# An output projection begun one block earlier beside a state-space scan, and GpSimd's pair addition kept to two blocks

## The chip, the core and the metric

The kernel runs on one core of a Trainium2 chip. The engines named here are TensorE (PE, matrix products; PEld are its weight loads), VectorE (DVE), ScalarE (ACT), GpSimd (POOL) and SyncE (SP), which issues most DMAs. Each works through its own instructions in the order in which the program gives them. The metric is device time of one execution in microseconds; lower is better.

## The reference

Four blocks follow each other on `x` of 2 x 512 rows of 512 numbers, each with a layer norm ahead and another behind, and a residual sum. Cut to the parts that matter here:

```python
x = x + ln(scan_block(ln(x)))      # the change is here
x = x + ln(gptq_ffn(ln(x)))        # ... and at the beginning of this
x = x + ln(attention(ln(x)))
x = x + ln(latent_ffn(ln(x)))

def scan_block(h):
    x, gate = split(h @ W_in.T)                    # 1024 channels each
    x = silu(causal_conv(x))
    ts, B, C = split(x @ W_x.T)                    # ranks: 32, 16, 16 wide, RMS-normed
    dt = softplus(ts @ W_dt.T + b_dt)
    state_t = state_{t-1} * exp(dt_t * A) + (dt_t * x_t) * B_t     # 16 states a channel
    y_t = sum_n(state_t * C_t)
    return ((y + x * D) * silu(gate)) @ W_out.T    # the output projection

def gptq_ffn(h):                                    # weights in 4 bits, 512 -> 1376 -> 512
    g, u = h @ Wg, h @ Wu
    return (silu(g) * u) @ Wd
```

## The kernel before

**Tiling.** A batch's 512 rows are four tiles of 128 rows (`TB` = 4) for norms and residual sums; for the scan, channels are on the partitions and time runs along the free axis. 2 batches of 8 channel blocks (`NCH` = 8, 128 channels each) make 16 blocks k; each has 8 steps gi (`NGI` = 8) of two states (`NG` = 2), so 128 steps s.

**Stages.** The first stage (to about 68 us) makes norms, projections and the convolution of batch 0. The second is the loop over s that is described next. The third (from L1180) projects batch 1's output, finishes the FFN of batch 0 and goes on to the rest of the model.

**A step of the scan.** VectorE multiplies (dt u) by B for two states (`times_B`, L1073) and runs the recurrence over 1024 elements (`scan`, L1077); ScalarE makes the decay factors two steps ahead (`exps`, L1057) in PSUM; GpSimd multiplies the states by C (`times_C`, L1083), and in the steps that `paired` names it adds the two states to each other (L1085). Two steps later TensorE sums the states into `y` in PSUM by products with the identity (`sums`, L1105): two products of 512 columns, or one where GpSimd has added already. Two steps into the next block VectorE multiplies `g` by `y` (`fin`, L1111). A product of 512 columns is two records of 0.43 us in the profile.

B and C of batch 1 are loaded step by step over block 7 (`states`, L560): each C tile is issued when GpSimd has read the buffer's last use by batch 0.

**The stream beside it.** Everything else that TensorE does in the second stage comes from one generator, `stream`: gates of batch 0, projections and ranks of batch 1, gates of batch 1, the product of two weight matrices of the last FFN (`fc1_expert`, stored to `wfe_d`), the output projection of batch 0 (`out_tiles`), the transposes of its norm (`turned`) and the FFN's first half (`ffn0`, 11 chunks of gate and up, 8 products each). Each step gives it a budget (`STEP` = 3.5 us, a product counts `MM` = 0.86) and takes products from it until that is used. `yield MM` ends a product; `until(key, lag)` holds the stream until an event lies `lag` half steps back. The clock `now` counts half steps (`tick`, two a step).

**Jobs.** What follows a product on the other engines is a job, given with `spawn(job, lag)` and advanced by `tick`; its `yield n` puts n half steps between its instructions. `bank` hands out the two PSUM buffers of the stream in turn, and `release` marks their last use. `pin` then fixes the order of TensorE, ScalarE, VectorE and GpSimd as it was written; SP's is the order of its DMAs in the program.

**The output projection.** For each tile i, 8 products over the blocks c go into one bank, with weights from four loads of 512 KB (`wo_pair`, L917; three buffers, shared with other weights). `out_job` evicts the bank, takes the moments (`add_normed`), normalizes, adds to `x` on GpSimd (L910), and `norm_one` starts the FFN's norm, whose result `turned` transposes for `ffn0`. `ffn_up_job` (L990) multiplies silu(gate) by up on VectorE.

In the third stage batch 1's projection (L1194) runs beside the dequantization of the down weights (`once`, L328 and L329, stored to `wd_d`), and the down projection (L1216) loads them from there.

Of the kernel before, what the change touches and what calls it, by code (L numbers as in the profile page):

```python
# [18 lines left out]
P = 128  # L19
# [4 lines left out]
TB = S // P  # L24
# [32 lines left out]
def tile_sandwich(  # L57
# [58 lines left out]
    def moments(srcs, name):  # L116

        mv = stat.tile([P, TB, 2], F32, tag="mv", name=f"mv_{name}")
        for i, s in enumerate(srcs):
            st = stat.tile([P, 6], F32, tag="st", name=f"st_{name}_{i}")  # L120
            nc.vector.bn_stats(st, s)
            nc.vector.bn_aggr(mv[:, i, :], st)
        return mv
# [304 lines left out]
    with ExitStack() as mamba:  # L428
# [254 lines left out]
        with ExitStack() as p2:  # L683
# [24 lines left out]
            def spawn(gen, lag=0):  # L708
                jobs.append([now[0] + lag, gen])
# [87 lines left out]
            def until(key, lag):  # L797
                while st.get(key, 1 << 30) + lag > now[0]:
                    yield None
# [32 lines left out]
            def turned(name, dst):  # L832

                for i in range(TB):
                    yield from until((name, i), 2)
                    tp = yield from bank(f"tp_{name}_{i}")
                    tp = tp.rearrange("p (k t) -> p k t", k=KH)
                    for kc in range(KH):
                        nc.tensor.transpose(tp[:, kc, :], st[name, i, "xn"][:, ts(kc, P)], ident)

                    def out(i=i, tp=tp):
                        nc.scalar.copy(dst[:, :, ts(i, P)], tp)
                        release(f"tp_{name}_{i}")
                        st[name, i, "free"] = st[name, "out"] = now[0]
                        yield 1

                    spawn(out(), 2)
                    yield MM / 2
                for i in range(TB):
                    while (name, i, "free") not in st:  # L850
                        yield None
# [31 lines left out]
                spawn(out(), 2)  # L883
                yield MM / 2

            def norm_one(b, i, name):

                mv = moments([xs(b)[i]], f"{name}_{i}")
                rs = rstd(mv, f"{name}_{i}", 1)
                nm = minus_mean(mv, rs, f"{name}_{i}", 1, True)  # L890
                yield 4
                xn = jrow(f"xn_{name}_{i}")
                apply(
                    xn.rearrange("p (k a r) -> p r k a", k=KH, a=2),
                    xs(b)[i].rearrange("p (r k a) -> p r k a", k=KH, a=2), rs, nm, 0,
                )
                st[name, i] = now[0]
                st[name, i, "xn"] = xn

            def add_normed(b, i, src, o):  # L900

# [13 lines left out]
            def wo_pair(b, i, j):  # L915
                w = wst.tile([P, 2, H], F32, tag="w4", name=f"wo{b}_{i}_{j}")
                nc.sync.dma_start(out=w, in_=w_out[j])  # L917
                return w

            def out_job(i, ps):  # L920
                o = jrow(f"o0_{i}")
                if i < TB - 1:
                    nc.scalar.copy(o, ps)
                    release(f"po0_{i}")
                    yield 3
                    yield from add_normed(0, i, o, o)
                else:
                    yield from add_normed(0, i, ps, o)
                    release(f"po0_{i}")
                yield 1  # L930
                yield from norm_one(0, i, "f0")

            def fc1_expert():

                fT = w4(fc1_wT.rearrange("p k (a n) -> p (k a) n", n=PW), "wf1T")
                fT = fT.rearrange("p (k a) n -> p k (a n)", k=LAT // P)
                ex = w4(expert_w, "wex", LAT // P, LAT)
                for a in range(KH // 2):
                    ps = yield from bank(f"pfe{a}")
                    for e in range(2):  # L940
                        for k in range(LAT // P):
                            nc.tensor.matmul(
                                ps[:, ts(e, LAT)], fT[:, k, ts(2 * a + e, P)], ex[:, k, :],
                                start=(k == 0), stop=(k == LAT // P - 1),
                            )
                        yield MM

                    def out(a=a, ps=ps):
                        t_ = trow(f"fe{a}")
                        nc.scalar.copy(t_, ps)  # L950
                        release(f"pfe{a}")
                        nc.sync.dma_start(
                            out=wfe_d[:, 2 * a : 2 * a + 2, :].rearrange("p k n -> p (k n)"), in_=t_
                        )
                        yield 1

                    spawn(out(), 2)

            def out_tiles():
                yield from until("fin7", 0)  # L960
                todo = [(i, j) for i in range(TB) for j in range(NCH // 2)]
                ws = {}
                for n, (i, j) in enumerate(todo):
                    for m in range(n, min(n + 2, len(todo))):
                        if m not in ws:
                            ws[m] = wo_pair(0, *todo[m])
                    if j == 0:
                        ps = yield from bank(f"po0_{i}")
                    for e in range(2):
                        c = 2 * j + e  # L970
                        nc.tensor.matmul(  # L971
                            ps, g[0][c][:, ts(i, P)], ws[n][:, e, :],
                            start=(c == 0), stop=(c == NCH - 1),
                        )
                        yield MM
                    if j == NCH // 2 - 1:
                        spawn(out_job(i, ps), 2)

            its = {}

# [29 lines left out]

            def stream():
                for c in range(1, NCH):
                    yield from gate(0, c)
                xT.append(xT_tile("xT1"))
                w_in(0, 1, 0)
                yield from turned("n1", xT[1])
                for c in range(NCH):
                    yield from proj_x(c)
                yield from until("words", 2)
                yield from gate(1, 0)  # L1020
                yield from gate(1, 1)
                yield from ranks1()
                yield from gate(1, 2)
                yield from gate(1, 3)
                yield from rows1()
                for c in range(NCH - 4, NCH):
                    yield from gate(1, c)
                yield from fc1_expert()
                yield from out_tiles()
                hTs["f", 0] = xT_tile("hT_f0")  # L1030
                yield from turned("f0", hTs["f", 0])
                yield from ffn0()
# [54 lines left out]
            def paired(s):  # L1087

                k, gi = divmod(s, NGI)

                return order[k][0] == 1 and (k - NCH not in (2, 3) and gi in (1, 5) or k - NCH < 2 and gi % 2 == 1)

            def sums(s):
                k, gi = divmod(s, NGI)
# [403 lines left out]
```

## Time and profile before

| | us |
|---|---|
| three runs | 945.83, 949.47, 949.53 (median 949.47) |
| the profiled execution | 946.45 |
| its span | 944.5 |
| first scan to the last scan's end | 68.0 to 562.1 |
| busy TensorE | 859.0 (91% of the span) |
| busy VectorE | 666.7 (71%) |
| busy GpSimd | 487.0 (52%) |
| busy ScalarE | 429.2 (45%) |
| mean granted clock of TensorE | 0.968 |

The first scans of the blocks from 6 on begin at 261.9, 292.0, 320.0 (block 8, the first of batch 1), 350.4, 386.4, 418.4, 447.5, 477.9, 506.9 and 536.5 us. The profile lists one execution; a line of the groups gives source line, engine, operation, tiles, count, then busy time, mean nanoseconds of one, and the idle time just before with what ended it. A row of the timeline has the start, the length, the engine, the line and the tiles, and in brackets the idle time before it and what was waited for. The windows give busy time (and instructions) of each engine in a stretch, then the granted clock of TensorE, the DMA share and GB/s.

### The profile page before, as it was taken

The page shows a single profiled execution, that of the slowest core. Times are in us where ns is not written, and L with a number is a line of the kernel's source. Part 1 is how long each engine was busy: PE and PEld are TensorE (multiplying, and loading weights), DVE is VectorE, ACT ScalarE, POOL GpSimd, SP SyncE. Part 2 cuts the span into 40 slices and gives each one's busy share as a digit, 9 for nine tenths or more (in the row PEclk, how much of TensorE's full clock was granted, in tenths as well). Part 3 has the DMA queues.
Part 4 walks back from the last instruction along what each step waited for, and adds up shares of the span by engine and source line. Part 5 has one row for each costly group of instructions (what it writes and reads, how often), then busy time and mean ns, then how long its engine had stood idle before and what let it go on. Part 6 is the DMA issues. An engine that isn't in the chain of part 4 may idle for free.

```text
span 944.5 us, 7179 instructions
## 1 busy us (share of the span) xinstructions
PE 859.0 (91%) x2188; PEld 384.5 (41%) x2188; DVE 666.7 (71%) x768; ACT 429.2 (45%) x655; POOL 487.0 (52%) x358
## 2 busy tenths in 40 slices
PE   6989979879999899579999999898999998999994
PEld 3434433323544343234434434344544444445441
DVE  5778999999999998999999986425600034535235
ACT  3368875655667645575565530215220014422122
POOL 7758887767887777866788783520000000011012
PEclk9989999989999899799999999999999999999998
DMA  6649100110004855000011114345212221200101
GB/s 195 207 135 375 38 30 31 38 38 25 21 25 169 287 173 158 25 0 23 22 44 45 31 32 145 132 138 200 67 57 88 59 90 44 67 12 23 56 0 44
DMA packets 43816, 80.08 MB, mean 85 GB/s; under 512 B 7774, under 2 KB 20937, under 8 KB 43778
## 3 DMA queue, kind: packets, MB, share of 16 engines
q1 hardware_dynamic: 41506, 73.64, 23.8%
q0 software_dynamic: 1984, 5.47, 1.6%
q10 hardware_dynamic: 288, 0.52, 0.2%
q8 instruction: 17, 0.28, 0.1%
q14 instruction: 21, 0.17, 0.1%
HBM read 68.37 MB, written 11.24 MB: 84 GB/s over the span
## 4 chain that ended last, share of the span: by engine, by line
PE 52%; DVE 25%; issue 8%; POOL 5%; ACT 4%; DMA 1%; DVEq 0%; POOLq 0%; SPq 0%; ACTq 0%
DVE bx L1077 9%; PE py L1105 8%; DVE bx L1073 7%; PE pd L1426 6%; PE pup L1363 5%; PE fo L1216 4%; PE fu L373 3%; PE fo L1279 3%; PE fg L373 3%; PE fu L1002 3%; PE po L1194 3%; PE fg L1002 3%; POOL bx L1083 3%; PE po L971 2%; DVE u L485 2%
## 5 line engine op out<-in xcount | busy, mean ns | idle before, releaser
L1083 POOL TENSOR_TENSOR bx<-bx,C 128x1024 f32<-128x1024 f32 x128 | 301.7, 2358 | 105.5 <-DVE bx L1077 84.2
L1077 DVE TENSOR_TENSOR_SCAN bx<-da,bx 128x1024 f32<-128x1024 f32 x128 | 292.1, 2283 | 0.3 <-ACT da L1057 0.2
L1105 PE MATMUL py<-bx,ident 128*128 128x512 f32 x480 | 233.7, 617 | 31.3 <-POOL bx L1083 26.6
L1057 ACT ACTIVATE da<-dt,A 128x511 f32<-128x511 f32 x256 | 176.4, 690 | 146.2 <-DVE bx L1077 140.3
L1073 DVE TENSOR_TENSOR bx<-du,B 128x1024 f32<-128x1024 f32 x127 | 153.4, 1209 | 3.6 <-POOL bx L1085 1.5
L1105 PEld LDWEIGHTS py<-bx,ident 128*128 128x128 f32 x480 | 90.9, 196 | 157.3 <-issue 93.6
L387 POOL TENSOR_TENSOR sd<-ve,half 128x4 f16<-128x4 f16 x2 | 2.1, 1042 | 110.7 <-DVE ve L385 110.7
L1292 DVE TENSOR_TENSOR it<-it,fu 128x512 f32<-128x512 f32 (+1 forms) x11 | 7.6, 687 | 72.3 <-PE fu L373 72.3
L1363 PE MATMUL pup<-hT_l,wup 128*128 128x512 f32 x128 | 57.8, 607 | 0.0
L749 PE MATMUL pg<-xT,w_g 128*128 128x512 f32 x114 | 56.2, 624 | 0.7 <-ACT dt L573 0.7
L1426 PE MATMUL pd<-wdn,hid 128*128 128x512 f32 x128 | 55.3, 592 | 0.0
L129 POOL TENSOR_TENSOR rs_lo<-ve_lo,mhalf 128x1 f32<-128x1 f32 x8 | 5.4, 680 | 76.7 <-DVE ve_lo L127 76.7
L1216 PE MATMUL fo<-wd,it 128*128 128x512 f32 (+1 forms) x88 | 39.7, 615 | 2.6 <-DMA wd<-wd_d 2.6
L1002 PE MATMUL fg<-hT_f,wg 128*128 128x512 f32 (+1 forms) x88 | 42.1, 597 | 0.0
L485 DVE SCALAR_TENSOR_TENSOR u<-px,ch,u 128x511 f32<-128x511 f32 (+2 forms) x48 | 35.9, 747 | 7.6 <-ACT u L478 6.5
L373 PE MATMUL fg<-hT_f,wg 128*128 128x512 f32 (+1 forms) x88 | 40.2, 593 | 0.7 <-ACT hT_f L173 0.7
L1002 PE MATMUL fu<-hT_f,wu 128*128 128x512 f32 (+1 forms) x88 | 40.7, 592 | 0.0
L373 PE MATMUL fu<-hT_f,wu 128*128 128x512 f32 (+1 forms) x88 | 39.8, 593 | 0.0
L1279 PE MATMUL fo<-wd,it 128*128 128x512 f32 (+1 forms) x88 | 39.6, 592 | 0.0
L1426 PEld LDWEIGHTS pd<-wdn,hid 128*128 128x128 f32 x128 | 24.2, 190 | 30.7 <-issue 30.1
L1291 ACT ACTIVATE it<-fg 128x512 f32<-128x512 f32 (+1 forms) x11 | 6.6, 597 | 65.7 <-PE fg L373 65.7
L1363 PEld LDWEIGHTS pup<-hT_l,wup 128*128 128x128 f32 x128 | 24.3, 193 | 28.8 <-issue 28.8
(242 smaller groups left out, 1165.8 us busy)
## 6 DMA issues: line engine op xcount, KB each, us to landing
wo<-in_W_outT SPq DMA_DIRECT2D x20, 512.0 KB
B<-scr SPq DMA_DIRECT2D x16, 512.0 KB
C<-scr SPq DMA_DIRECT2D x16, 512.0 KB
wg<-wgu_d SPq DMA_DIRECT2D x10, 512.0 KB
wu<-wgu_d SPq DMA_DIRECT2D x10, 512.0 KB
w_x<-in_W_in SPq DMA_DIRECT2D x8, 512.0 KB
wgu_d<-w_gu POOLq DMA_DIRECT2D x16, 256.0 KB, 2.4
w_g<-in_W_in SPq DMA_DIRECT2D x8, 512.0 KB
```

The source lines that it names most:

```text
L373: nc.tensor.matmul(ps[:m], w[:, kc, e * P : e * P + m], hT[:, kc, :], start=(kc == 0), stop=(kc == KH - 1),)
L749: nc.tensor.matmul(ps, w[:, k, ts(e, P)], xT[b][:, k, :], start=(k == 0), stop=(k == KH - 1))
L1002: nc.tensor.matmul(ps[:m], wt[j][a][:, kc, e * P : e * P + m], hT[:, kc, :], start=(kc == 0), stop=(kc == KH - 1),)
L1057: nc.scalar.activation(das[s % 2][:, i, 1:], st["dt", b, c][:, 1:], AF.Exp, scale=A[:, c, n : n + 1])
L1073: nc.vector.tensor_mul(bx, st["du"].unsqueeze(1).to_broadcast([P, NG, S]), Bbs[b][gi])
L1077: nc.vector.tensor_tensor_scan(flat, das[s % 2].rearrange("p n t -> p (n t)"), flat, 0.0, ALU.mult, ALU.add)
L1083: nc.gpsimd.tensor_mul(bxs[s], bxs[s], Cbs[b][s % NGI])
L1105: nc.tensor.matmul(st["y"], ident, bx[:, i, :], start=False, stop=last)
L1216: nc.tensor.matmul(fo[t], its[i][:m, ts(t, P)], w[:m, e], start=(i == 0), stop=(i == len(IC) - 1),)
L1279: nc.tensor.matmul(fo[t], its[i][:m, ts(t, P)], w[:m], start=(i == 0), stop=(i == len(IC) - 1),)
L1363: nc.tensor.matmul(ps, w[:, kc, ts(e, P)], src[kc], start=(kc == 0), stop=(kc == KH - 1))
L1426: nc.tensor.matmul(pd, hid[kc][:, ts(i, P)], wdn[kc], start=(kc == 0), stop=(kc == INT // P - 1),)
```

## The change

It has four parts, all in the second stage:

1. `fc1_expert` and its stores move from behind the gates of batch 1 to behind those of batch 0; its weights are loaded by `fc1_weights` one gate earlier.
2. The output projection of batch 0 starts when block 6 is finished (`fin6`), not block 7. Tile 1 goes first, over blocks 0 to 6, in a bank `pp0_1` that ScalarE copies to `po0_part`; then tile 0, whose last product waits for `fin7`; then tile 1's part is brought back by a product with the identity and block 7 is added. Tiles 2 and 3 follow.
3. Tiles 2 and 3 go through `late_tile`: the moments are read from PSUM, the lags between the instructions are shorter, and the sum with `x` is on VectorE. In `turned`, the lag for these tiles is 1 half step rather than 2.
4. `paired` names the odd steps of blocks 8 and 9 alone. Before, it also named steps 1 and 5 of blocks 12 to 15.

```diff
             def turned(name, dst):
                 for i in range(TB):
-                    yield from until((name, i), 2)
+                    lag = 1 if name == "f0" and i >= TB - 2 else 2
+                    yield from until((name, i), lag)
                     tp = yield from bank(f"tp_{name}_{i}")
                     tp = tp.rearrange("p (k t) -> p k t", k=KH)
                     for kc in range(KH):
...
                         st[name, i, "free"] = st[name, "out"] = now[0]
                         yield 1
-                    spawn(out(), 2)
+                    spawn(out(), lag)
                     yield MM / 2
                 for i in range(TB):
                     while (name, i, "free") not in st:
...
                 spawn(out(), 2)
                 yield MM / 2
-            def norm_one(b, i, name):
-                mv = moments([xs(b)[i]], f"{name}_{i}")
-                rs = rstd(mv, f"{name}_{i}", 1)
-                nm = minus_mean(mv, rs, f"{name}_{i}", 1, True)
-                yield 4
+            def spread_out(b, i, name, rs, nm):
                 xn = jrow(f"xn_{name}_{i}")
                 apply(
                     xn.rearrange("p (k a r) -> p r k a", k=KH, a=2),
...
                 )
                 st[name, i] = now[0]
                 st[name, i, "xn"] = xn
+            def norm_one(b, i, name):
+                mv = moments([xs(b)[i]], f"{name}_{i}")
+                rs = rstd(mv, f"{name}_{i}", 1)
+                nm = minus_mean(mv, rs, f"{name}_{i}", 1, True)
+                yield 4
+                spread_out(b, i, name, rs, nm)
             def add_normed(b, i, src, o):
...
                 nc.sync.dma_start(out=w, in_=w_out[j])
                 return w
+            def late_tile(i, ps, o):
+                mv = moments([ps], f"mo0_{i}")
+                rs = rstd(mv, f"mo0_{i}", 1)
+                nm = minus_mean(mv, rs, f"mo0_{i}", 1, True)
+                yield 2
+                apply(o, ps, rs, nm, 0)
+                release(f"po0_{i}")
+                yield 1
+                nc.vector.tensor_add(xs(0)[i], xs(0)[i], o)
+                mv = moments([xs(0)[i]], f"f0_{i}")
+                rs = rstd(mv, f"f0_{i}", 1)
+                nm = minus_mean(mv, rs, f"f0_{i}", 1, True)
+                yield 2
+                spread_out(0, i, "f0", rs, nm)
             def out_job(i, ps):
                 o = jrow(f"o0_{i}")
-                if i < TB - 1:
-                    nc.scalar.copy(o, ps)
-                    release(f"po0_{i}")
-                    yield 3
-                    yield from add_normed(0, i, o, o)
-                else:
-                    yield from add_normed(0, i, ps, o)
-                    release(f"po0_{i}")
+                if i >= TB - 2:
+                    yield from late_tile(i, ps, o)
+                    return
+                nc.scalar.copy(o, ps)
+                release(f"po0_{i}")
+                yield 3
+                yield from add_normed(0, i, o, o)
                 yield 1
                 yield from norm_one(0, i, "f0")
-            def fc1_expert():
+            def fc1_weights():
                 fT = w4(fc1_wT.rearrange("p k (a n) -> p (k a) n", n=PW), "wf1T")
                 fT = fT.rearrange("p (k a) n -> p k (a n)", k=LAT // P)
-                ex = w4(expert_w, "wex", LAT // P, LAT)
+                return fT, w4(expert_w, "wex", LAT // P, LAT)
+            def fc1_expert(fT, ex):
                 for a in range(KH // 2):
                     ps = yield from bank(f"pfe{a}")
                     for e in range(2):
...
                     spawn(out(), 2)
             def out_tiles():
-                yield from until("fin7", 0)
-                todo = [(i, j) for i in range(TB) for j in range(NCH // 2)]
+                yield from until(f"fin{NCH - 2}", 0)
+                todo = [(i, j) for i in (1, 0, *range(2, TB)) for j in range(NCH // 2)]
                 ws = {}
+                def add(ps, i, c, w, start=False):
+                    nc.tensor.matmul(
+                        ps, g[0][c][:, ts(i, P)], w[:, c % 2, :],
+                        start=start, stop=(c == NCH - 1 - (i == 1 and "part" not in st)),
+                    )
+                def part_out(ps):
+                    part = st["part"] = new_u("po0_part")
+                    nc.scalar.copy(part, ps)
+                    release("pp0_1")
+                    st["parted"] = now[0]
+                    yield 1
                 for n, (i, j) in enumerate(todo):
                     for m in range(n, min(n + 2, len(todo))):
                         if m not in ws:
                             ws[m] = wo_pair(0, *todo[m])
                     if j == 0:
-                        ps = yield from bank(f"po0_{i}")
-                    for e in range(2):
-                        c = 2 * j + e
-                        nc.tensor.matmul(
-                            ps, g[0][c][:, ts(i, P)], ws[n][:, e, :],
-                            start=(c == 0), stop=(c == NCH - 1),
-                        )
+                        ps = yield from bank(f"pp0_{i}" if i == 1 else f"po0_{i}")
+                    for c in (2 * j, 2 * j + 1):
+                        if c < NCH - 1:
+                            add(ps, i, c, ws[n], start=(c == 0))
+                            yield MM
+                    if j < NCH // 2 - 1:
+                        continue
+                    if i == 1:
+                        spawn(part_out(ps), 2)
+                        continue
+                    yield from until(f"fin{NCH - 1}", 0)
+                    add(ps, i, NCH - 1, ws[n])
+                    yield MM
+                    spawn(out_job(i, ps), 2)
+                    if i == 0:
+                        yield from until("parted", 0)
+                        ps = yield from bank("po0_1")
+                        nc.tensor.matmul(ps, ident, st["part"], start=True, stop=False)
                         yield MM
-                    if j == NCH // 2 - 1:
-                        spawn(out_job(i, ps), 2)
+                        add(ps, 1, NCH - 1, ws[n])
+                        yield MM
+                        spawn(out_job(1, ps), 2)
             its = {}
...
             def stream():
                 for c in range(1, NCH):
+                    if c == NCH - 1:
+                        fw = fc1_weights()
                     yield from gate(0, c)
                 xT.append(xT_tile("xT1"))
                 w_in(0, 1, 0)
+                yield from fc1_expert(*fw)
                 yield from turned("n1", xT[1])
                 for c in range(NCH):
                     yield from proj_x(c)
...
                 yield from rows1()
                 for c in range(NCH - 4, NCH):
                     yield from gate(1, c)
-                yield from fc1_expert()
                 yield from out_tiles()
                 hTs["f", 0] = xT_tile("hT_f0")
                 yield from turned("f0", hTs["f", 0])
...
                 k, gi = divmod(s, NGI)
-                return order[k][0] == 1 and (k - NCH not in (2, 3) and gi in (1, 5) or k - NCH < 2 and gi % 2 == 1)
+                return NCH <= k < NCH + 2 and gi % 2 == 1
             def sums(s):
                 k, gi = divmod(s, NGI)
```

## Prediction, made before the changed kernel was run

> **What bounds the kernel now.** The busy table gives TensorE 91% of the span and VectorE 71%, but the 40 slices show VectorE at 9 tenths from about 140 to 540 us, where the scan runs. The groups say what a step of the scan holds:
>
> ```profile
> L1077 DVE TENSOR_TENSOR_SCAN bx<-da,bx 128x1024 f32<-128x1024 f32 x128 | 292.1, 2283 | 0.3 <-ACT da L1057 0.2
> ...
> L1073 DVE TENSOR_TENSOR bx<-du,B 128x1024 f32<-128x1024 f32 x127 | 153.4, 1209 | 3.6 <-POOL bx L1085 1.5
> ```
>
> Scan and times_B together are 3.49 us by the means; successive scans start 3.31 us apart (records overlap a little), so a block of 8 steps with its du (0.87) and fin (0.6) takes 27.95 us. Next, what VectorE itself waits for between 68 and 562 us (the view of waits: total, times, longest):
>
> ```profile
> DVE g L1111 <- PE py L1105: 4.5, 2, 3.4
> DVE du L1071 <- ACT du L1065: 2.7, 2, 1.9
> DVE st_f L121 <- POOL x L910: 1.9, 2, 1.5
> DVE it L990 <- PE fu L1002: 1.8, 2, 1.3
> DVE bx L1073 <- POOL bx L1085: 1.5, 1, 1.5
> ```
>
> Under 13 us of 494: **the scan is VectorE-bound**, and each microsecond put on VectorE, or each new wait of VectorE, moves the end of the scan. The change can win these waits, or lose by new ones. Last, the timeline where block 7 ends and the output projection begins (start, length, instruction; SPq is the load queue):
>
> ```profile
> 317.35 1.98 PE L1105 MATMUL py<-bx,ident 128*128 128x512 f32 x4 [0.79 <-POOL bx L1083]
> ...
> 321.53 0.32 SPq L560 DMA_DIRECT2D C<-scr  x1
> 321.55 3.66 PE L1105 MATMUL py<-bx,ident 128*128 128x512 f32 x4 [2.22 <-POOL bx L1083]
> ...
> 325.52 0.66 DVE L1111 TENSOR_TENSOR g<-g,py 128x512 f32<-128x512 f32 x1
> ...
> 327.86 4.51 PE L971 MATMUL po<-wo,g 128*128 128x512 f32 x6 [1.59 <-DMA wo<-in_W_outT]
> ```
>
> The last C tile of batch 1 goes out at 321.53, when GpSimd has read the buffer for the last time; the first `wo` is right behind it in SP's queue (321.94) and is used at 327.86. The fin of block 7, at 325.52, waits for nothing.
>
> **A. The early start: +6.3.** In the changed order, tile 1's projection over blocks 0 to 6 (7 products) fills TensorE in block 7, where it idles; then comes tile 0's first product, and only behind it the last two `sums` of block 7. SP takes its queue in order: B and C tiles of batch 1 now stand between the `wo` loads, and the load for tile 0 still stands behind the last C. It therefore issues at about 321.9 as before and lands at about 328.2 (327.7 before by its semaphore, and I add 0.5 because two 512 KB loads replace two 256 KB stores ahead of it). TensorE is in order, so the last `sums` of block 7 wait for a load that they do not need. Then 0.86 us for tile 0's product (two records of 0.43) and 1.72 for the sums, plus 0.2 to drain: fin of block 7 at 331.0. Behind fin on VectorE stand times_B and the scan of block 8, then ScalarE's exponentials and GpSimd's products. 331.0 is +5.5.
>
> Here the clock decides the rest. The row at 321.55 took 3.66 us for four records which took 1.98 at 317.35, after 2.22 us idle, and the windows give
>
> ```profile
> 320.00:325.00 5.00, 3.45 (x4) 1.18 (x4) 5.00 (x4) 3.05 (x4) 3.85 (x2) 0.66 0.93 290
> ```
>
> with a granted clock of 0.66 (third number from the end). The Trainium skill, "TensorE: Matmul & The Clock Gate", section "Part 1: The HAM clock gate", has half clock after an idle window of about 3.4 us; the new wait, from about 323 to 328.2, is longer than that, the old 2.22 is not and yet it was followed by half clock. So the row is the stricter. By full clock +5.5; with both products at half clock 328.2 + 1.7 + 3.66 = 333.6, +8.1. I take +6.3, fin at 331.8.
>
> **B. Waits that go: -4.5.** The 1.47 (times_B behind GpSimd's pair addition at 337.6) and the 3.42 (fin of block 8, at 360.27) exist because TensorE came late into block 8. From 328.2 it has 35 products to the last `sums` of block 8, before 36 from 327.86, so it gets there at about 360.1 again; fin of block 8 is due at 360.27 - 3.42 - 1.47 + 6.3 = 361.7. Both waits go, -4.9. The moments of tile 2, now read from PSUM with a shorter lag, wait some 0.4. Both ends: -4.9 and 0.
>
> **C. Residual additions of tiles 2 and 3 from GpSimd to VectorE: +0.6.** Two 128x512 additions at 0.65 (fin's row, 0.66) are +1.3. The trace has no such addition in the scan, with both inputs in SBUF: du, y and the exponentials are in PSUM. The nearest rows are from the dequantization:
>
> ```profile
> 582.55 0.68 DVE L328 TENSOR_TENSOR w_d<-q_d,z_d 128x512 f32<-128x512 int32 x1
> ...
> 583.31 1.39 POOL L329 TENSOR_TENSOR w_d<-w_d,s_d 128x512 f32<-128x512 f32 x1 [0.96 <-DVE w_d L328]
> ...
> 583.60 1.65 DVE L328 TENSOR_TENSOR w_d<-q_d,z_d 128x512 f32<-128x512 int32 x1
> ```
>
> Alone 0.68; begun inside a GpSimd operation of 1.39 it ends just after it (585.25 against 584.70). The rule that speaks against the change is in "SBUF — State Buffer", section "SBUF: two separate sides": VectorE with two SBUF inputs and GpSimd share a port pair as an exclusive lock, and the second blocks for all of the first's instruction. The row agrees in kind. By the row each addition loses 1.0; by the rule, against GpSimd's times_C of 2.36 us, up to 2.4 each; nothing if GpSimd is idle there, as it is some 20% of this stretch. I take 0.6 each, the low side since the step's order lets times_C finish first: +1.2. The waits of VectorE's norms on GpSimd's additions go, -1.9. Range -0.6 to +4.2.
>
> **D. One more FFN product inside the scan, and its waits: +5.4.** Everything comes 8 half steps earlier, so ten of eleven `it` products run on VectorE inside the scan, not nine: +0.6. What these wait for is the greater part. Before, one fu product finishes in the same step as the `it` that reads it, and it costs:
>
> ```profile
> 464.10 1.21 DVE L1073 TENSOR_TENSOR bx<-du,B 128x1024 f32<-128x1024 f32 x1
> ...
> 466.62 0.69 DVE L990 TENSOR_TENSOR it<-it,fu 128x512 f32<-128x512 f32 x1 [1.31 <-PE fu L1002]
> ```
>
> A second (436.18, one step of lag) costs 0.50. In the changed order five (numbers 0, 2, 7, 8, 9) stand in the step of their last product. Four at about 1.1 and the first at 2.2 (TensorE starts the FFN cold) are 6.6, less the 1.8 measured: +4.8. This holds while TensorE has no lead, and it has none: the first 10 FFN blocks, the sums and projections from block 10 on are 193 products, 193 x 0.859 = 165.8 us, beside about 170 us of VectorE. The 8 pair additions taken from GpSimd put 8 x 0.86 = 6.9 us of it there. GpSimd's 8 x 1.26 = 10.1 us saved are worth nothing: with 82% busy from 480 to 562 it is not late. Were TensorE one step ahead, the waits would be gone, -1.8; if all `it` waited, +7.
>
> **E. fc1 and its stores moved from block 7 to block 1: -0.5.** Eight products of half width (3.4 us) into a stretch with TensorE at 83% from 120 to 170 us: hidden by its idle time. They let the gates slide into later gaps (1.65 us at 238) and may ease two waits of 1.09 and 0.86 at 268 and 287. Its two loads ride on an SP queue that is empty there. Range -2 to +0.5.
>
> **F. After the scan: -1.3.** Only one FFN product is left behind the last `sums`, six before: 4.3 us less in
>
> ```profile
> 568.15 1.88 PE L1002 MATMUL fg<-hT_f,wg 128*96 128x512 f32 x4
> ...
> 569.87 3.60 PE L1002 MATMUL fu<-hT_f,wu 128*96 128x512 f32 x8
> ...
> 599.89 0.96 SPq L1211 DMA_DIRECT2D wd<-wd_d  x2
> 603.58 3.40 PE L1216 MATMUL fo<-wd,it 128*128 128x512 f32 x5 [2.65 <-DMA wd<-wd_d]
> ```
>
> But the down projection starts at 603.58 on a load, not on TensorE: its weights are dequantized first, by VectorE and GpSimd behind the last fin, stored and loaded again. That chain hangs on the scan's end, so TensorE mostly waits longer in its place (2.65 becomes 6 to 7), and at half clock. Less SP traffic ahead of it may bring up to 2 us; one `it` product now stands ahead of it, 0.7. Ends -4.3 and +1.5.
>
> **Sum**: 6.3 - 4.5 + 0.6 + 5.4 - 0.5 - 1.3 = +6.0 on the profiled execution's 946.45 (span 944.5), 952.5. The three runs have median 949.47 and mean 948.3, so the same sum there is 955.5 and 954.3; I take 954.
>
> **Rivals.** *TensorE keeps one step of lead*: the products of D find their results ready (-1.8 + 0.6 in place of +5.4), A and B stay, C is 0.6: +6.3 - 4.5 + 0.6 - 1.2 - 0.5 - 1.3 = -0.6 to +1, so 948 to 950. For it: TensorE's idle time in block 7 is used; against it: D's 98%. *Faster, by the freed waits and tail*: if tile 0's load lands before the last C is due, A is under 2 and the 4.3 us of F are won in full: 2 - 4.5 - 0.6 - 1.2 - 0.5 - 4.3 = -9, 940. It decides once fin of block 7 waits under 2 us and the down projection moves ahead by 4 us against the scan's end. Against it: SP's order, and 2.65 us of wait already before 603.58. *Worse, TensorE becomes the bound from block 10*: half clock after cold starts and waits for weights make fins wait 1 to 3 us in several blocks, as the one at 360.27; about +6 more: 960. *That it does not do what it says* is out by the built order: the products do stand 8 half steps earlier.
>
> **How the numbers follow.** Forecast 0.49 (950 to 958), TensorE ahead 0.24 (946 to 951), faster 0.13 (938 to 944), worse 0.14 (957 to 964). A half percent, 4.7 us, is about what a measurement of this kernel tells from no change: slower 0.58 (0.44 of the forecast and the worse case), within it 0.29 (TensorE ahead and 0.05 of the forecast), faster 0.13. The range leaves the outer parts of the last two out: 945 to 961.
>
> **What would show it.** A: fin of block 7 with a wait of 5 to 8 us on `py`, TensorE's wait before it on a DMA of `wo`. B: no wait over 0.5 at block 8's fin. C: two additions of 0.7 to 2.4 us. D: five waits of about 1 us of `it` on `fu`. F: the down projection starts 40 to 42 us after the last scan's end (41.5 before), with a wait of over 5 us. The prediction is wrong if fin of block 7 starts before 328, or if `it` products wait under 2 us in all.

## The result and the profile after

| | us |
|---|---|
| the changed kernel | median 963.35 of 6 (959.38 to 965.93) |
| before, on the same chip | median 949.5 of 6 (945.83 to 953.15) |
| ratio | 1.0145, 95% interval 1.0124 to 1.0166 |
| profiled execution | 964.32 (span 962.5, clock 0.966); before 946.45 (944.5, 0.968) |

The change makes the kernel 1.45% slower, 13.8 us by the medians. The two profiled executions are 17.9 us apart; the one before lies 3.0 us under the median of its kernel and the one after 1.0 over, which is the difference. The account below is of these two.

The last scan ends at 580.25, before at 562.08; from there to the end it is 382.3 us, before 382.4. So the loss arose in the scan. Its 18.3 us there divide by VectorE's records, each counted from the end of the one before it, into 13.9 of waits, 2.5 for the two additions to `x`, 1.0 for one more `it` product and 0.9 of small parts. In the rows, `it` is VectorE's product of silu(gate) with `fu`, TensorE's result of the up projection; `py` is the bank in which `sums` makes `y`, and `st_f` and `st_mo` are first steps of the norms. VectorE's waits in the changed kernel, 68 to 575 us (total, times, longest):

```profile
DVE g L1162 <- PE py L1156: 10.4, 3, 8.5
DVE it L1039 <- PE fu L1051: 9.0, 5, 3.7
DVE du L1122 <- ACT du L1116: 2.8, 2, 1.9
DVE it L1039 <- POOL bx L1134: 1.8, 1, 1.8
DVE x L933 <- ACT o L152: 1.4, 1, 1.4
```

The rows of GpSimd's pair addition (1.5) and of `st_f` behind GpSimd's `x` (1.9) are gone. What waits now is fin on `py` and the FFN's `it` on `fu`; the fourth row is one of these too, for `fu` and GpSimd's product ended within 0.02 us of each other there, and the view names the later, which `it` does not read. The first of these is at the end of block 7, in the timeline:

```profile
321.66 0.32 SPq L560 DMA_DIRECT2D C<-scr  x1
322.07 4.58 SPq L921 DMA_DIRECT2D wo<-in_W_outT  x3
...
329.65 1.24 PE L988 MATMUL po<-wo,g 128*128 128x512 f32 x2 [3.40 <-DMA wo<-in_W_outT]
330.69 3.47 PE L1156 MATMUL py<-bx,ident 128*128 128x512 f32 x4
...
334.20 0.69 DVE L1162 TENSOR_TENSOR g<-g,py 128x512 f32<-128x512 f32 x1 [8.46 <-PE py L1156]
```

The load for tile 0 stands behind the last C, TensorE's first product of tile 0 waits 3.40 us for it, the sums behind it run at half clock (3.47 for four records, 1.88 at 322.78), and fin, which waited for nothing before, waits 8.46. In the view of the chain that ended last, this load takes from its issue to its landing

```profile
322.07 7.45 DMA wo<-in_W_outT
```

and the first one behind the last C took, in the kernel before,

```profile
321.94 5.79 DMA wo<-in_W_outT
```

The windows show how full the DMA engines were meanwhile, and the clock behind it:

```profile
325.00:330.00 5.00, 1.47 (x3) 0.59 (x4) 0.74 (x1) 3.15 (x4) 3.61 (x3) 1.00 1.01 370
330.00:335.00 5.00, 5.00 (x8) 1.50 (x6) 0.80 (x2) 0.00 (x0) 0.00 (x0) 0.66 0.07 26
```

In the first the DMA engines are full (share 1.01, 370 GB/s; before 0.84 and 322); in the second the clock is 0.66 and VectorE is busy 0.80 of 5 us. The `it` products wait longest at the first of them and in block 14:

```profile
418.45 1.02 PE L1051 MATMUL fu<-hT_f,wu 128*128 128x512 f32 x2
...
419.58 0.69 DVE L1039 TENSOR_TENSOR it<-it,fu 128x512 f32<-128x512 f32 x1 [3.70 <-PE fu L1051]
...
537.64 0.69 DVE L1039 TENSOR_TENSOR it<-it,fu 128x512 f32<-128x512 f32 x1 [3.02 <-PE fu L1051]
```

At 419.58 the product starts just behind its last two records of fu: it reads what TensorE ends in the same step. The two additions to `x`, with GpSimd's work beside them:

```profile
369.45 1.81 POOL L914 TENSOR_TENSOR x<-x,o 128x512 f32<-128x512 f32 x1
369.47 0.67 DVE L933 TENSOR_TENSOR x<-x,o 128x512 f32<-128x512 f32 x1
...
388.05 2.34 POOL L1134 TENSOR_TENSOR bx<-bx,C 128x1024 f32<-128x1024 f32 x1
...
388.98 1.97 DVE L933 TENSOR_TENSOR x<-x,o 128x512 f32<-128x512 f32 x1 [1.42 <-ACT o L152]
```

The first takes 0.67 and GpSimd's addition beside it 1.81 (the same addition takes 1.27 at 375.28); the second begins inside a GpSimd product and takes 1.97, after a wait of 1.42 for ScalarE. After the scan the down projection starts 38.9 us behind the scan's end (before 41.5):

```profile
615.39 0.96 SPq L1262 DMA_DIRECT2D wd<-wd_d  x2
...
619.13 7.39 PE L1267 MATMUL fo<-wd,it 128*128 128x512 f32 x11 [4.46 <-DMA wd<-wd_d]
```

It still waits for its weights, now 4.46 us. The latent FFN's down product starts 266.7 us after the scan's end (before 268.0), and its 128 products are busy for 56.5 us rather than 55.3 with the same instructions; most of what the tail had won was lost there; why is not shown.

### The profile page after: what moved, and what is told of

The parts are those of the page before. It is cut to its first block, busy times and chain, and to the rows that moved or that the text cites. A ratio compares the mean times of both kernels' runs of the same rounds, so it can differ in the third digit from the quotient of the medians.

```text
span 962.5 us, 7190 instructions
## 1 busy us (share of the span) xinstructions
PE 867.7 (90%) x2206; PEld 388.1 (40%) x2206; DVE 672.2 (70%) x770; ACT 429.4 (45%) x655; POOL 475.3 (49%) x348
## 4 chain that ended last, share of the span: by engine, by line
PE 50%; DVE 23%; issue 9%; POOL 6%; ACT 4%; DMA 2%; SPq 1%; DVEq 0%; POOLq 0%; ACTq 0%
PE py L1156 10%; DVE bx L1128 8%; PE pd L1477 6%; DVE bx L1124 6%; PE pup L1414 5%; PE fo L1267 4%; PE fu L373 3%; PE fo L1330 3%; PE fg L373 3%; POOL bx L1134 3%; PE fu L1051 3%; PE pg L749 2%; DVE u L485 2%; PE fg L1051 2%; PE po L988 1%
## 5 line engine op out<-in xcount | busy, mean ns | idle before, releaser
L1156 PE MATMUL py<-bx,ident 128*128 128x512 f32 x496 | 239.9, 612 | 30.9 <-POOL bx L1134 29.0
L1156 PEld LDWEIGHTS py<-bx,ident 128*128 128x128 f32 x496 | 93.0, 194 | 157.6 <-issue 92.4
L1477 PE MATMUL pd<-wdn,hid 128*128 128x512 f32 x128 | 56.5, 602 | 0.0
L1051 PE MATMUL fu<-hT_f,wu 128*128 128x512 f32 (+1 forms) x88 | 44.0, 617 | 1.1 <-ACT dt L573 1.1
L373 PE MATMUL fu<-hT_f,wu 128*128 128x512 f32 (+1 forms) x88 | 39.8, 593 | 0.0
```

The lines of the kernel that those rows point to most:

```text
L373: nc.tensor.matmul(ps[:m], w[:, kc, e * P : e * P + m], hT[:, kc, :], start=(kc == 0), stop=(kc == KH - 1),)
L1051: nc.tensor.matmul(ps[:m], wt[j][a][:, kc, e * P : e * P + m], hT[:, kc, :], start=(kc == 0), stop=(kc == KH - 1),)
L1156: nc.tensor.matmul(st["y"], ident, bx[:, i, :], start=False, stop=last)
L1477: nc.tensor.matmul(pd, hid[kc][:, ts(i, P)], wdn[kc], start=(kc == 0), stop=(kc == INT // P - 1),)
```

## The experiments

Each is the changed kernel or the kernel before with the edit shown; times are medians with the ratio to the kernel before on the same chip (the changed kernel's is 1.0145, 1.0124 to 1.0166). Of two profiles, differences of some 2 us say little: block 0 of the scan, whose code is the same in the changed kernel and in experiments 1 to 6, 9 and 11, lasts 31.5 us in four of their profiles and 33.2 to 33.4 in five. Where the scan's length is compared, it is therefore from block 1 on.

**1. Tile 0 begins with weights that are there.**

```diff
+ if n == NCH // 2:
+     add(ps, i, NCH - 2, ws[n - 1], start=True)
+     yield MM
  for c in (2 * j, 2 * j + 1):
-     if c < NCH - 1:
-         add(ps, i, c, ws[n], start=(c == 0))
+     if c < NCH - 1 and (i, c) != (0, NCH - 2):
+         add(ps, i, c, ws[n], start=(c == 0 and i != 0))
```

> The changed kernel, but tile 0 begins with block 6, whose weights are the pair that tile 1 has just used, instead of block 0, whose load is still to come. The same loads and the same number of products. Theory (the last sums of block 7 wait behind a load they do not need): the wait of block 7's fin falls from 8.5 us to 3 to 4 (tile 1's own last load, landing at about 325, still stands ahead), nothing takes its place at once, and the time falls by about 5 us, ratio to the kernel before 1.009. Rival (TensorE is the bound of what follows, so that the stall only pays its debt earlier): fin's wait falls as well, but waits of `it`, of the moments or of later fins grow by as much, and the time falls by less than 2 us.

Measured: 958.41, ratio 1.0108 (1.0079 to 1.0136), 4.9 us less by the medians. The timeline at the same place:

```profile
324.29 1.02 PE L988 MATMUL pp<-wo,g 128*128 128x512 f32 x2
325.15 1.02 PE L988 MATMUL po<-wo,g 128*128 128x512 f32 x2
326.01 1.88 PE L1159 MATMUL py<-bx,ident 128*128 128x512 f32 x4
327.82 1.12 PE L568 MATMUL pv<-dtT,wdt 33*128 33x512 f32 x2
327.92 0.69 DVE L1165 TENSOR_TENSOR g<-g,py 128x512 f32<-128x512 f32 x1 [2.16 <-PE py L1159]
```

TensorE does not stop, the clock stays full (1.88 for the sums), and fin waits 2.16, less than the 3 to 4 expected. The `it` waits sum to 9.5, 10.8 in the changed kernel: they did not grow, so the stall had paid no debt of TensorE's. The interval touches that of the changed kernel; the cause is read from the wait, and the scan from block 1 on is 7.9 us shorter.

**2. The pair additions back.** `paired` as before the change.

> The changed kernel with the pair additions of GpSimd in steps 1 and 5 of blocks 12 to 15 put back (8 products of 0.86 us less on TensorE, 8 additions of 1.26 more on GpSimd). Theory (TensorE has no slack from block 12 on): the waits of `it` after 480 us, 5.3 us in the changed kernel, fall under 2.5, those of blocks 10 and 11 (5.5) stay, and the time falls by 3 to 5 us. Rival (the waits come from where the `it` products stand against their last fu product, not from the number of products): the sum of the waits of `it` stays within 1.5 us of 10.8 and the time within 1.5.

Measured: 963.29, ratio 1.0143 (1.011 to 1.0176). No gain by the medians. VectorE's waits from 100 to 565 us:

```profile
DVE g L1162 <- PE py L1156: 9.7, 3, 7.8
DVE it L1039 <- PE fu L1051: 9.1, 5, 3.9
```

The `it` waits sum to 9.1, not 10.8, a little beyond what the rival allowed, and those after 480 us to 3.5, not under 2.5: with less work on TensorE the products moved to other steps, in blocks 12 and 13 two waits of 1.20 came, and in block 14 the 3.02 went. The scan from block 1 on is 2.1 us shorter, within what two profiles differ by. The theory, 3 to 5 us, falls; where `it` stands weighs more here than the number of products.

**3. The additions read PSUM.**

```diff
- apply(o, ps, rs, nm, 0)
- release(f"po0_{i}")
+ apply(ps, ps, rs, nm, 0)
  yield 1
- nc.vector.tensor_add(xs(0)[i], xs(0)[i], o)
+ nc.vector.tensor_add(xs(0)[i], xs(0)[i], ps)
+ release(f"po0_{i}")
```

> The changed kernel, with ScalarE writing the normalized tiles 2 and 3 back into their PSUM bank and VectorE adding them to x from there, so that VectorE's two additions have one input in SBUF rather than two. Theory (the second addition took 1.97 us because it shared a port with a GpSimd product that ran from 388.05 to 390.39): both additions take 0.65 to 0.70 whatever GpSimd does beside them, about 1.3 us less. Rival (it is long for another reason, such as x coming straight from a load or from ScalarE): one of them stays over 1.2. The bank is held a half step longer, which may move tile 3 and the FFN by a step; the durations of the two additions decide, not the total.

Measured: 958.49, ratio 1.0103 (1.0074 to 1.0131). The additions and what runs beside them:

```profile
372.51 1.28 POOL L914 TENSOR_TENSOR x<-x,o 128x512 f32<-128x512 f32 x1
372.52 0.66 DVE L932 TENSOR_TENSOR x<-x,po 128x512 f32<-128x512 f32 x1
...
394.56 0.66 DVE L932 TENSOR_TENSOR x<-x,po 128x512 f32<-128x512 f32 x1
394.79 2.36 POOL L1134 TENSOR_TENSOR bx<-bx,C 128x1024 f32<-128x1024 f32 x1 [1.48 <-DVE bx L1128]
```

Beside GpSimd at the same place as before, 0.66 and 1.28 in place of 0.67 and 1.81: with one input in PSUM neither holds up the other. The second has a GpSimd product begin 0.23 us into it, which keeps its 2.36; none was running when it started, so this run does not repeat the case of the 1.97. The total cannot be put down to the additions: with the later release of the bank tile 3 and the FFN moved as well, the wait on ScalarE went, and the waits of `it` on `fu` are 2.18, 0.58, 1.38, 2.11, 0.62 and 1.33.

**4. The `it` products later.**

```diff
- spawn(job(i, ps), 2)
+ spawn(job(i, ps), 2 + 2 * a)
```

> The changed kernel with the job that multiplies silu(gate) by up on VectorE started 4 half steps after its last fu product was issued, not 2. Theory (VectorE waits because the `it` product stands in the step of its last fu product): the waits of `it`, 10.8 us in six places, fall under 3 and the time falls by 6 to 9 us. Rival (TensorE is short of time from block 10 on, so the wait only shows where VectorE first needs a result): the waits come back at fin of the blocks 10 to 15 on py, together with what remains at `it` over 8 us, and the time falls by less than 3.

Measured: 953.18, ratio 1.0039 (1.0024 to 1.0054), 10 us less. The waits from 300 to 570 us:

```profile
DVE g L1162 <- PE py L1156: 10.7, 3, 8.8
DVE x L933 <- ACT o L152: 1.4, 1, 1.4
DVE it L1039 <- PE fu L1051: 0.7, 1, 0.7
```

Of 10.8 us of `it` waits 0.7 remain, and those of fin in blocks 10 to 15 do not grow (the 10.7 are 8.8 of block 7, 1.4 of block 9 and 0.6 of block 6). TensorE had the time; VectorE asked one step too early.

**5 and 6. The edits of experiments 1, 3 and 4 together, with the pairs as before the change and as after it.**

> The changed kernel with the three single edits together (tile 0 from block 6, the additions from PSUM, the it products 4 half steps after their last fu product) and with the pair additions in blocks 12 to 15 put back. Theory (the waits are separate and add up): 963.4 less 5.0, 4.9 and 10.2 is 943, and as the edits share some waits (the one before the addition, the it waits which the addition's edit also moved) 944 to 949, ratio 0.995 to 1.000, with under 7 us of waits in the scan beyond those before block 7. Rival (TensorE is the bound once the waits are out): the scan ends no earlier than with the it edit alone, at 570 or later, with waits of fin on py in blocks 12 to 15, and the time stays at 951 or above.

> As the run with the three edits and the pairs put back, but with the pairs as the changed kernel has them: 8 more products on TensorE in blocks 12 to 15. Theory (the pairs did not matter where the waits hid it): within 1 us of the run with the pairs put back, or 1 to 3 slower because TensorE now has to do these products. Rival (TensorE bound): 4 to 7 us slower than it.

Measured: 946.0 and 946.15, ratios 0.9971 (0.9954 to 0.9988) and 0.997 (0.9957 to 0.9982). Both are a little faster than the kernel before; the single gains (5, 5 and 10 us) would have given 943, so they share a part. The largest waits of experiment 6 from 100 to 565 us:

```profile
DVE g L1165 <- PE py L1159: 5.3, 3, 2.8
DVE du L1125 <- ACT du L1119: 0.9, 1, 0.9
```

There `it` waits for nothing, and the 8 products on TensorE cost nothing that shows.

**7. The kernel before with `it` later.** The edit of experiment 4.

> The kernel before with one edit, the it products 4 half steps after their last fu product. Theory (each microsecond that VectorE waits in the scan is a microsecond of the end): its two waits of it (0.50 and 1.31) go, -1 to -2 us, ratio 0.998 to 0.999. Rival: the bank of fu is held longer and the FFN is delayed, so that more is left after the last scan: 0 to +2 us.

Measured: 948.03, ratio 0.9985 (0.9972 to 0.9998). The two waits go, one of 0.88 comes at 530.6, and 8 products of the FFN are left after the last sums, not 6.

**8. The kernel before with the change's pair rule.**

> The kernel before with the change's pair rule alone: the additions of two states in blocks 12 to 15 move from GpSimd to TensorE. Theory (as the run with the pairs put back showed, they move neither the waits nor the time): within 1.5 us of before, ratio 0.9985 to 1.0015, with some 5 to 8 products more of the FFN left after the last scan. Rival (as the prediction had it, 6.9 us put on a full engine): +3 to +6 us, as waits of it or as a later start of the down projection.

Measured: 953.87, ratio 1.0046 (1.0029 to 1.0062): the theory falls here. VectorE's waits from 100 to 565 us:

```profile
DVE it L990 <- PE fu L1002: 4.9, 4, 2.5
```

They were 1.8. In this kernel the 8 products delay fu enough that `it` waits 1.75 at 500.3 and 2.46 at 563.5: 3.1 us more, of the 4.7 by which the two profiled executions differ. Part 4 thus has no fixed price: next to nothing in experiments 2 and 6, 4.6 us by the medians here, most of it where a fu product comes late to its reader.

**9. Experiment 6 with one more edit: fin of block 7 first.**

```diff
+ if n == NCH // 2 - 1:
+     yield from until(f"fin{NCH - 1}", 0)
```

> The run with the three edits (pairs as in the changed kernel) and one more: tile 1's product with block 6 is held until block 7's fin has been issued, so that no product of the projection stands between TensorE and the last sums of block 7. Theory (each load that stands ahead of the sums on TensorE is a wait of fin): the wait of block 7's fin, 2.8 us there, falls under 0.5 and the time by 2 to 3 us, ratio to before about 0.994 to 0.995. Rival (TensorE then comes late into block 8): waits of times_B or of block 8's fin of 1.5 to 4 us appear, as in the kernel before, and the time stays within 1 us of 946.

Measured: 944.63, ratio 0.9954 (0.9942 to 0.9966). Fin of block 7 waits for nothing (2.81 without this edit); but the moments of tile 2 wait 1.67 (0.51), the fin of block 10 2.29 (1.89), and a scan waits 0.64 for ScalarE. Most of the wait came back, as the rival had it though at other places; the scan from block 1 on is 0.3 us shorter. The medians are 1.5 us apart, on different chips and with intervals that overlap, so no gain is shown.

**10. The kernel before with the fc1 part alone.** `fc1_weights` and the earlier call, as in the change's diff, and nothing else.

> The kernel before with the change's first part alone: the products of fc1 with the experts' matrix and their two stores behind the gates of batch 0, in block 1. Theory (they fill idle time of TensorE there): waits in blocks 0 to 6 change by less than 1 us in all, nothing else moves, ratio 0.999 to 1.001. Rival (with block 7 emptied, the stores no longer stand ahead of the first projection weights, which land earlier): the waits at block 8 (1.5 and 3.4 us) shrink by 1 us or more, ratio 0.997 to 0.999.

Measured: 943.45, ratio 0.9937 (0.9919 to 0.9956): 5.9 us faster. Both waits at block 8 (1.47 and 3.42) are gone. In its timeline

```profile
274.26 0.38 SPq L917 DMA_DIRECT2D wo<-in_W_outT  x1
...
300.07 0.38 SPq L917 DMA_DIRECT2D wo<-in_W_outT  x1
...
320.98 0.39 SPq L917 DMA_DIRECT2D wo<-in_W_outT  x1
324.55 0.32 SPq L560 DMA_DIRECT2D C<-scr  x1
...
328.55 0.66 DVE L1115 TENSOR_TENSOR g<-g,py 128x512 f32<-128x512 f32 x1
```

three `wo` loads are issued before the last C, the first 54 us ahead of fin. The fc1 weights use the same three buffers; with them gone early, the loads go out when the buffers are free, past the B and C tiles. In the kernel before all of them stand behind the last C (321.94). In the code `out_tiles` asks for them after `fin7` and so after every B and C load: `pin` leaves SP out, and SP's queue in the built program is not in the order of the code. The rival holds, with more than its number. Tile 0's products then need not wait for a load; the first row is of this run, the second of the kernel before, the last two of experiment 7:

```profile
327.54 5.42 PE L973 MATMUL po<-wo,g 128*128 128x512 f32 x12
...
327.86 7.08 PE L971 MATMUL po<-wo,g 128*128 128x512 f32 x12 [1.59 <-DMA wo<-in_W_outT]
...
325.42 1.98 PE L1105 MATMUL py<-bx,ident 128*128 128x512 f32 x4 [2.22 <-POOL bx L1083]
...
331.49 7.08 PE L971 MATMUL po<-wo,g 128*128 128x512 f32 x12 [3.03 <-DMA wo<-in_W_outT]
```

Here TensorE begins tile 0 4.5 us after the first scan of block 8 (7.9 in the kernel before) and does twelve records at full clock, 1.66 us sooner. In experiment 7 the last sums of block 7 ran at full clock; the load was then waited for 3.03, half clock followed, and fin of block 8 waited 3.42 again. So it is the late load, and the half clock behind it, that made TensorE late into block 8.

By the profiles the scan from block 1 on is 4.6 us shorter and the stretch behind it 1.0, but the first stage and block 0 are 2.7 longer; so the two spans differ by 2.9 us, the medians by 5.9, and only the 4.6 have a cause shown.

**11. The edits of experiments 1 and 4 without that of 3: the additions read SBUF again.**

> The run with the three edits (pairs as in the changed kernel), with VectorE's two additions taken back to both inputs in SBUF: tile 0 from block 6 and the it products later remain. Theory (the shared port costs 1.4 us on one addition and ScalarE's normalization is not ready for it, 1.4 us): 2.5 to 3.5 us slower than the three edits together, 949. Rival (a wait on VectorE there is absorbed by a later one, such as the fin of block 9 with its 1.4 us): within 1 us of 946.

Measured: 944.28, ratio 0.995 (0.9932 to 0.9968), not slower than experiment 6. The second addition and the product beside it:

```profile
383.71 0.69 DVE L933 TENSOR_TENSOR x<-x,o 128x512 f32<-128x512 f32 x1 [0.43 <-ACT o L152]
383.78 2.83 POOL L1137 TENSOR_TENSOR bx<-bx,C 128x1024 f32<-128x1024 f32 x1
```

Here VectorE came 0.07 us ahead: its addition takes 0.69, and GpSimd's product 2.83 rather than 2.36. Which of the two pays depends here on who comes first, and the kernel's time shows no price.

**12. The two edits that help the kernel before, those of 7 and 10.**

> The kernel before with the two single edits that made it faster, fc1 in block 1 (which let two loads of the projection's weights go ahead of the last C tiles) and the it products 4 half steps after their last fu product. Theory (waits of VectorE in the scan add up): -5.9 and -1.3 us, some 942, ratio 0.991 to 0.993, with under 1 us of it waits. Rival (TensorE, freed of its late start, is now ahead at the it products, or more of the FFN is left after the scan): no faster than fc1 alone, ratio 0.993 to 0.995.

Measured: 943.07, ratio 0.9939 (0.9923 to 0.9955), as fc1 alone. The scan is shorter (490.0 us from its first start, 491.1 with fc1 alone), but 8 products of the FFN instead of 6 are left behind it. The rival holds.

## Why the prediction failed

The forecast was slower by 6 us, in a range of 945 to 961; it is slower by 14. The steps that failed are the sizes of the two largest terms: D, +5.4, measured +9.9, and A, +6.3, measured +8.5. The measured terms below add up to 16.9 of the 17.9 us between the two profiles. The waits that D and A named are those found; the ground given for D was not the right one, and B's waits go without part 2.

- **D, the terms that failed most**: +5.4 predicted, +9.9 in the profiles. The five places named (0, 2, 7, 8, 9) did wait, and a sixth (5, 0.58). They are 3.70, 1.76, 3.02, 0.60 and 1.10 instead of 2.2 and four times 1.1; of the 1.81 of before nothing is left, so +9.0 net, and +1.0 for the product. One wait of 1.31 was too thin a base: the five waits measured 0.60 to 3.70, by how late TensorE came in each step. The prediction's ground, that TensorE has no lead because it is 98% full, is not what costs: experiment 4 gave TensorE no time, and the waits went.
- **A, the term that was mis-sized**: +6.3, measured +8.5. The order of events is as predicted. The load landed 1.3 us later than estimated (329.5, not 328.2): the 0.5 us allowed for two 512 KB loads in place of two 256 KB stores was too little in a stretch with full DMA engines. And the sums ran at half clock after a wait of 3.40 us, 3.47 us in place of 1.88, where I had taken a value near the full one. The same wait is 3.35 to 3.53 us in experiments 2, 3 and 4, and half clock followed each time. After shorter gaps it did not follow always: the 2.22 us from which the prediction read a stricter rule stand at the same place in experiments 7 and 8, and the four records behind them took 1.98 and 2.63 there, not 3.66. My upper end, +8.1 with both products at half clock, was near in its sum, though only the sums were slow and the load was later.
- **B**: -4.5, measured -4.3 (1.47 and 3.42 gone, 0.58 new at the moments). A fin on `py` of block 9 that waits 1.36 was not foreseen. The prediction put them down to TensorE's late start into block 8, which holds, and their end to tile 1's early products, which were not needed: experiment 10 shows that part 1 alone takes both waits away.
- **C**: +0.6, measured +2.0. The additions' own 2.55 us is what I had (2.5), but that is in part luck: I had each lose 0.6, and one took 0.67 and the other, which began inside `times_C` against the order that I had assumed, 1.97. The wait of 1.42 on ScalarE was missed, a new wait in place of the removed 1.93.
- **E**: -0.5, measured -0.4 up to 300 us. What I missed is SP's queue later on: part 1 alone makes the kernel before 5.9 us faster. In the changed kernel tile 1 takes these early loads (issued at 271.38, 297.18, 314.57 and 318.11), so tile 0's falls behind the last C again: by the timelines, part 2 spends what part 1 wins.
- **F**: -1.3, measured -2.6 at the start of the down projection and -1.3 at the last FFN's down product, -0.2 at the end. That the down projection waits for its weights and not for the FFN's last products was right; its wait, forecast at 6 to 7, is 4.46.

Of the rivals, "TensorE keeps one step of lead" fell with the 10.8 us of `it` waits and the faster one with fin's 8.46; "worse" (960) came nearest in time, but by the forecast's own waits and not by TensorE becoming the bound. One reading of the prediction is off, with nothing resting on it: the slices show VectorE at nine tenths from 94 us, not from 140.

What stays open: the last 1.0 of the 17.9 us, what of the 5.9 of experiment 10 lies outside the 4.6 shown, and why the stretch behind the scan is 2.8, 1.0 and 2.2 us shorter in experiments 9, 10 and 11 than in the kernel before, and 0.8 longer in 12. No run has parts 2 and 3 without each other or without part 1's buffers, so their single prices are read from waits alone. Experiment 10's kernel is among the best shown, beside experiments 9, 11 and 12, whose intervals overlap with it.

## What to carry to other kernels

Filler that is put ahead of critical work on an in-order engine makes that work wait for the filler's operands: put first what is already loaded. A reader on the bound engine wants a step between it and the end of its producer; asking a step later gave 10 us in the changed kernel, where removing 7 us of TensorE's work gave nothing by the medians. And read what a moved piece sets free: buffers that come free early let later loads pass in the queue, which took away two waits of 4.9 us where part 1 had been expected to bring 0.5.

## What was not expected of the hardware

An addition with both inputs in SBUF beside GpSimd holds up one of the two: VectorE's went from 0.67 to 1.97 when GpSimd's product had been running for 0.9 us, GpSimd's from 2.36 to 2.83 when VectorE's had begun 0.07 us ahead, and from 1.27 to 1.81 when both records begin within 0.02 us (GpSimd's first). The second addition took 1.95, 1.93 and 1.94 in experiments 1, 2 and 4 too, each time begun some 0.95 us into a GpSimd product. With one input in PSUM both kept their times (0.66 and 1.28). That GpSimd could be the one to pay was not in the forecast. That is the lock of the Trainium skill's "SBUF — State Buffer", section "SBUF: two separate sides": the one that starts first holds the ports. The trace agrees for starts that lie apart (the addition of 1.97 ended at 390.95, GpSimd's product at 390.39); at 0.02 us the order of the records does not tell who held them.
